# A sample's best eight found once for both halves, four gathers for eight, and the experts' first product two groups ahead

## The chip, the cores and the metric

The kernel runs on one core of a Trainium2 chip. The metric is the device time in microseconds (us) of one execution. Where the traces speak of engines, PE is TensorE (PEld its weight loads), DVE VectorE, ACT ScalarE, POOL GpSimd, and SP the engine whose queue issues most DMAs. All arithmetic is float32.

## What is computed

The input is x of 4 samples, 128 channels, 64 x 64 pixels (4096 tokens of 128 features a sample). Layer 0 normalises, makes three 1x1 convolutions and one attention over the 4096 pixels. Layer 1 first adds an attention that is a running softmax over the tokens, and then a feed-forward with 64 experts, each of which chooses its own tokens. This last part is what the change is about:

```python
logits = einsum('bsd,ed->bse', x, gate_w) + gate_b
probs = softmax(logits, axis=1)                      # over the 4096 tokens
vals, idx = top_k(probs.transpose(0, 2, 1), 8)       # each expert takes 8 tokens
gathered = take x at idx                             # (sample, 8, expert, 128)
pooled = einsum('bked,bke->bed', gathered, topv)
h = gelu([pooled, 1] @ weight1[e])                   # 128 -> 512
out = [h, 1] @ weight2[e]                            # 512 -> 128
outputs.at[idx].add(out * topv)                      # back to the chosen tokens
```

x is here the normalised token stream, and the result is added to the stream. The two weight matrices of an expert are 256 KB each, 32 MB for all 64.

## The kernel before

**Stages.** Layer 0 (its lines lie beyond L1730) fills the first 1530 us or so. Then `loop` goes over 32 blocks of 512 tokens (8 a sample) and does the running attention of one block per turn; in each turn slots named 1, 2, "D", 3, 4, "T" and "G" are places where other work is inserted. `make_plan` (from L2034) writes down by hand what goes where: the second normalisation of a finished block (`gate_norm`), its transposition (`gate_turn`), its logits (`gate_logits`), and the choice of a sample's tokens once its eight blocks are through. After the loop follow `last_choice` (for the last sample, whose last block is only just ready), `experts` (16 groups of 4 experts), and `stores`. TensorE, DVE, ACT and POOL execute in the order in which the program is written; SP executes its DMAs in the order written too, and each waits there until its target may be overwritten and until the eighth DMA before it has landed.

**A sample's choice.** The logits of a sample lie as 128 partitions x 2048: partition h x 64 + e holds expert e over one half h of the tokens. `gate_logits` (L1285 to L1293) takes the best eight of each block with the MAX8 instruction. `merge_half` (L1308) takes the best eight of those, per partition. `merge_halves` gives each partition the other half's eight: one matmul with a permutation, `swap`, exchanges the partition halves (f_pw, L1314); MAX8 over the sixteen gives the eighth best of the whole sample, the threshold, and the greatest (f_neg, L1320). `candidate_rows` searches the partition's own eight in its 2048 logits (L1326) and turns their places into row numbers of the sample's table in DRAM (L1328). `gathers` fetches them: one indirect DMA on POOL's queue for each k of 0 to 7, one row per partition (L1334). All of a half's eight are fetched, though some of them don't belong to the sample's best eight; `weigh_candidates` (L1374) gives those the weight zero. `spread_candidates` (L1382) lays the weights out as eight 128 x 64 matrices, and `pool` multiplies the eight gathered tiles with them on TensorE, accumulating (f_pp, L1406).

**The plan around it.** For the first two samples the search and the exchange stand in one turn of the loop, and the gathers go out in it and the four turns after it, at most two in a row on POOL. For the third sample there are only three turns left: its gathers stand in seven places of turns 29 to 31, four of them back to back on POOL. For the last sample, all eight stand in the last turn's "T", ahead of the outputs of the last block (L1192) on DVE. POOL makes the weight tiles of the running attention too (L1092 to L1113), once a turn.

**`last_choice`** (from L1436) fills TensorE with transpositions of earlier blocks of the stream (`fill`, L1422), which ACT or DVE copy back (`put_back`, L1434), while it normalises the last block, makes its logits, merges its best eight with the earlier ones, and pools (L1489 to L1500). It ends with the division by the softmax's sum (L1507 to L1519), which gives `pooled`.

**`experts`** keeps 21 experts' weights in the rooms that the loop has given up. For each group of four it makes the first product (`first`, f_ph, L1628), ACT copies it (f_hr, L1632), TensorE transposes it (`turn`, L1639), DVE adds the bias, ACT applies the Gelu, and the second product follows (`second`, f_eo, L1657). `first` and `second` reload what they have read (`reload1` L1564, `reload2` L1571). `turn_back` (L1589) transposes further blocks of the stream in between. The order is first(0); then for each g: turn(g), one or two turn_backs, first(g+1), second(g).

## Time and profile before

| what | us |
|---|---|
| median of 3 runs | 2319.7 (2317.64 to 2321.2) |
| the profiled execution's own time | 2321.39 |
| its span, first to last instruction | 2319.7 |
| DVE busy | 1440.9 |
| POOL busy | 193.5 |
| DMA moved | 105.82 MB |

The profile is of one execution. Its page names the busy time of each engine, a chain of work that ended last (followed back from the last instruction to what released each step), and groups of instructions by source line. Other views of the same trace list the chain by time, the instructions by time (start, duration, engine, line, output <- inputs, and in brackets how long the engine was idle before and what ended that), and busy times by stretch. "remote" in brackets, "another core or an unknown queue" in the chain, stands for a wait whose release the profile cannot put down to an instruction or a DMA that ended then.

### The profile page before, as it was taken

How to read it: one execution, taken by the hardware profiler on the slowest of the kernel's cores; microseconds unless marked ns; L12 is line 12 of the kernel's file. 1: busy time of each engine (PE TensorE's matmuls, PEld its weight loads, DVE VectorE, ACT ScalarE, POOL GpSimd, SP SyncE). 2: the span in 40 equal slices, each digit the busy share in tenths (PEclk: the TensorE clock that was granted, in tenths of full speed). 3: DMA queues.
4: the chain of work that ended last, by engine and by line, in shares of the span. 5: the costliest groups of instructions: out<-in, count | busy, mean ns of one | idle time of the engine just before them, and what ended most of it. 6: DMA issues, size and time to landing. Idle time of an engine off the chain costs nothing.

```text
span 2319.7 us, 43135 instructions
## 1 busy us (share of the span) xinstructions
PE 2247.9 (97%) x18354; PEld 1171.3 (50%) x18354; DVE 1440.9 (62%) x2325; ACT 1085.9 (47%) x1322; POOL 193.5 (8%) x364
## 2 busy tenths in 40 slices
PE   7999999999999999999999999999999999999887
PEld 3644444444444444444444444455655655656553
DVE  7666565655665565565556656567777777874533
ACT  2343334433333443334454544445665666665641
POOL 0000000000000000000000000002212222223411
PEclk9999999999999999999999999999999999999999
DMA  2100010000010000001000000011111121124578
GB/s 70 39 12 16 9 45 8 17 8 9 13 48 9 9 17 8 9 13 39 9 5 5 8 7 5 20 44 35 47 58 49 48 63 46 52 61 130 177 250 306
DMA packets 79067, 105.82 MB, mean 46 GB/s; under 512 B 9232, under 2 KB 45072, under 8 KB 78864
## 3 DMA queue, kind: packets, MB, share of 16 engines
q1 hardware_dynamic: 77264, 99.81, 14.0%
q8 instruction: 146, 2.39, 0.4%
q0 software_dynamic: 1024, 2.10, 0.4%
q10 hardware_dynamic: 576, 1.05, 0.1%
q14 instruction: 57, 0.47, 0.1%
HBM read 79.60 MB, written 17.04 MB: 42 GB/s over the span
## 4 chain that ended last, share of the span: by engine, by line
PE 88%; DVE 4%; ACT 3%; DMA 3%; issue 1%; another core or an unknown queue 1%; SPq 0%; POOL 0%; ACTq 0%; DVEq 0%; POOLq 0%
PE av L1901 37%; PE sc L1876 19%; PE f_pv L1128 9%; PE f_pk L973 8%; PE f_pt L1151 3%; PE f_po L1174 2%; PE pd L1927 1%; PE pa L1849 1%; PE pe L1823 1%; PE f_po L1186 1%; ACT f_e1a L980 1%; PE f_pl L1285 1%; DMA x<-in_x_dram 1%; PE otr L1939 1%
## 5 line engine op out<-in xcount | busy, mean ns | idle before, releaser
L1901 PE MATMUL av<-pr,am 64*128 64x512 f32 x4096 | 979.0, 592 | 1.7 <-ACT pr L1881 1.7
L1881 ACT ACTIVATE pr<-sc 128x1024 f32<-128x1024 f32 x512 | 524.2, 1024 | 783.4 <-PE sc L1876 773.5
L1888 DVE TENSOR_TENSOR acc<-acc,pr 128x1024 f32<-128x1024 f32 x480 | 586.8, 1222 | 486.7 <-ACT pr L1881 482.5
L1901 PEld LDWEIGHTS av<-pr,am 64*128 64x128 f32 x4096 | 402.6, 187 | 472.0 <-issue 458.4
L1876 PE MATMUL sc<-e,e 64*128 64x512 f32 x2048 | 536.6, 593 | 3.9 <-DMA e<-side 3.9
L1876 PEld LDWEIGHTS sc<-e,e 64*128 64x128 f32 x2048 | 202.4, 188 | 236.2 <-issue 230.3
L1128 PE MATMUL f_pv<-f_held,f_ama 128*32 128x256 f32 x4096 | 238.1, 381 | 7.0 <-ACT f_e1a L980 4.6
L973 PE MATMUL f_pk<-f_held,f_ama 128*128 128x512 f32 x512 | 234.9, 603 | 0.0
L1133 ACT ACTIVATE f_amb<-f_pv 128x1024 f32<-128x1024 f32 x128 | 130.8, 1024 | 126.3 <-PE f_pv L1128 124.2
L981 DVE TENSOR_TENSOR f_e1a<-f_e1a,f_held 128x1024 f32<-128x1024 f32 x128 | 157.0, 1228 | 48.1 <-ACT f_e1a L980 47.8
L980 ACT ACTIVATE f_e1a<-f_pk 128x1024 f32<-128x1024 f32 x128 | 130.0, 1025 | 119.3 <-PE f_pk L973 54.6
L1128 PEld LDWEIGHTS f_pv<-f_held,f_ama 128*32 128x32 f32 x4096 | 129.7, 110 | 101.4 <-issue 11.9
L982 DVE TENSOR_REDUCE f_e1a<-f_e1a 128x8 f32<-128x1024 f32 x128 | 155.3, 1218 | 3.5
L973 PEld LDWEIGHTS f_pk<-f_held,f_ama 128*128 128x128 f32 x512 | 92.5, 190 | 108.6 <-issue 101.0
L1092 POOL COPY f_held<-f_e1a 32x32 f32<-32x32 f32 x128 | 30.9, 242 | 898.2 <-DVE f_e1a L1074 560.7
L918 POOL MEMSET f_held<- 128x1024 f32 x1 | 1.0, 957 | 1037.2 <-DVE xn L1814 1037.2
L1151 PE MATMUL f_pt<-f_amb,f_held 128*32 128x128 f32 x1920 | 83.7, 278 | 0.6 <-ACT f_amb L1133 0.6
L1151 PEld LDWEIGHTS f_pt<-f_amb,f_held 128*32 128x32 f32 x1920 | 60.4, 110 | 10.3 <-issue 5.2
L1192 DVE TENSOR_TENSOR t<-t,f_po 128x512 f32<-128x512 f32 (+1 forms) x33 | 22.1, 671 | 64.2 <-PE f_po L1186 55.5
L956 ACT ACTIVATE f_xl<-t,ln_nb,ln_rs 128x128 f32<-128x128 f32 x128 | 52.8, 491 | 0.8 <-PE pa L1849 0.8
L1266 ACT ACTIVATE f_x<-t,f_gnb,f_grs 128x128 f32<-128x128 f32 x126 | 51.3, 483 | 0.4 <-DVE f_gnb L1247 0.4
L1885 DVE COPY acc<-pr 128x1024 f32<-128x1024 f32 x32 | 22.2, 694 | 39.3 <-ACT pr L1881 39.3
(275 smaller groups left out, 1789.6 us busy)
## 6 DMA issues: line engine op xcount, KB each, us to landing
f_e2a<-f_rd SPq DMA_DIRECT2D x128, 128.0 KB
xr<-in_xtok_dram SPq DMA_DIRECT2D x32, 256.0 KB
f_table<-f_x SPq DMA_DIRECT2D x62, 128.0 KB
out_dram<-t SPq DMA_DIRECT2D x14, 512.0 KB
x<-in_x_dram SPq DMA_DIRECT2D x12, 512.0 KB
e<-e SPq DMA_DIRECT2D x32, 128.0 KB
f_ama<-f_rd SPq DMA_DIRECT2D x16, 256.0 KB
f_e1b<-f_rd SPq DMA_DIRECT2D x16, 256.0 KB
```

The costliest lines, as they stand in the source:

```text
L956: nc.scalar.activation(xl[:, c, :], t[:, b * NCH + i, :], AF.Identity, bias=ln_nb[:, b, i : i + 1], scale=ln_rs[:, b, i : i + 1],)
L973: nc.tensor.matmul(pk[:, i, :], xt_at(n)[:, bass.ts(c, P)], env.wks[:, bass.ts(i, BLK)], start=True, stop=True,)
L980: nc.scalar.activation(flat, pk.rearrange("p i x -> p (i x)"), AF.Silu)
L981: nc.vector.tensor_mul(ks, ks, env.qb)
L982: nc.vector.tensor_reduce(s[:, (n % GB) * CPB + c, :], ks, AX.X, ALU.add)
L1128: nc.tensor.matmul(pv[a * CH : (a + 1) * CH, i, :], xt_at(m)[:, bass.ts(c * NA + i, CH)], env.wvs[:, bass.ts(a, HH * C)], start=True, stop ...
L1133: nc.scalar.activation(env.amb[:, bass.ts(c, HD)], pv.rearrange("p i x -> p (i x)"), AF.Silu)
L1151: nc.tensor.matmul(env.pt[i * CH : (i + 1) * CH, :], lhs, rhs, start=i not in env.begun, stop=False, skip_group_check=True,)
L1876: nc.tensor.matmul(sc[:, u, :], e2[halves[u], p, :], e1[halves[u], cols], start=True, stop=True,)
L1881: nc.scalar.activation(pr, sc, AF.Exp)
L1888: nc.vector.tensor_add(acc, acc, pr)
L1901: nc.tensor.matmul(av, am[h, j, :], pr[h, u, :], start=(j == 0), stop=(j == NCH - 1))
```

## The change

**The choice.** The row numbers are now searched before the exchange. The exchange carries values and row numbers of both halves: four matmuls with halves of the identity (`both_halves`) put both halves' sixteen values and sixteen row numbers on each partition. There MAX8 and its index search find the sample's best eight and their places among the sixteen, so both partitions of an expert know all eight; the lower partition takes the first four, the upper the last four. The row numbers of these four are picked out by comparing the places with the constants 0 to 15 (`spare(3, 48, 16)`, filled once by POOL with sixteen memsets) and summing the matches. So each partition gathers four rows, and `spread_candidates` and `pool` handle four tiles.

**The plan.** For the first three samples the search takes the slot before, and the exchange the slot after, compared with the order of the two before. The gathers of samples 0 and 1 are one a turn; sample 2's stand in four places. In `last_choice` put_back(8) and put_back(5) go from DVE to ACT, and the matmul of the softmax's sum (f_pq) is issued after the first half of the last pooling matmuls.

**The experts.** first(0) and first(1) come ahead of the loop over groups, and first(g+2) takes the place of first(g+1). f_hr, of which there was one, has two places by turns.

```diff
         def merge_half(b, count):
             st = sel[b]
-            st["both"] = both = small_tile(b, "both", 24, bufs=1)
+            st["both"] = both = small_tile(b, "both", 16, bufs=1)
             nc.vector.max(out=both[:, 0:8], in_=st["cand"][:, : count * 8])
+        def both_halves(tile_, what):
+            pw = sm(what, 2, tile_.shape[1])
+            for h in range(2):
+                for to in range(2):
+                    nc.tensor.matmul(
+                        pw[to * E : (to + 1) * E, h], ident[:, h * E : (h + 1) * E], tile_,
+                        start=True, stop=True,
+                    )
+            return pw
+        def candidate_rows(b, count):
+            st = sel[b]
+            both = st["both"]
+            ci = small_tile(b, "ci", 8, dtype=U32, bufs=1)
+            nc.vector.max_index(out=ci, in_max=both[:, 0:8], in_values=flat_lg(b, 0, count))
+            nc.vector.tensor_scalar(
+                out=both[:, 8:16], in0=ci, scalar1=env.base[:, b : b + 1], scalar2=None,
+                op0=ALU.add,
+            )
         def merge_halves(b):
             st = sel[b]
-            both = st["both"]
-            pw = sm(f"f_pw_{b}", 8)
-            nc.tensor.matmul(pw, env.swap, both[:, 0:8], start=True, stop=True)
-            nc.vector.tensor_copy(both[:, 8:16], pw)
-            st["top"] = top = small_tile(b, "top", 8)
-            nc.vector.max(out=top, in_=both[:, 0:16])
-            nc.vector.tensor_copy(both[:, 16:17], top[:, 7:8])
+            pw = both_halves(st["both"], f"f_pw_{b}").rearrange("p s (v k) -> p v s k", v=2)
+            found = spare(3, 0, 32).rearrange("p (v s k) -> p v s k", v=2, s=2)
+            nc.vector.tensor_copy(found, pw)
+            first8 = spare(3, 32, 16).rearrange("p (v k) -> p v k", v=2)
+            st["top"] = top = first8[:, 0]
+            vals, rows16 = spare(3, 0, 16), spare(3, 16, 16)
+            nc.vector.max(out=top, in_=vals)
             st["neg"] = neg = small_tile(b, "neg", 1)
             nc.vector.tensor_scalar_mul(neg, top[:, 0:1], -1.0)
+            pos = small_tile(b, "ci", 8, dtype=U32, bufs=1)
+            nc.vector.max_index(out=pos, in_max=top, in_values=vals)
+            nc.vector.tensor_copy(first8[:, 1], pos)
+            st["own"] = own = small_tile(b, "own", 2, 4, bufs=1)
+            for h in range(2):
+                half = slice(h * E, (h + 1) * E)
+                nc.vector.tensor_copy(own[half], first8[half, :, 4 * h : 4 * h + 4])
+            st["src"] = src = small_tile(b, "src", 5, bufs=1)
+            nc.vector.tensor_copy(src[:, 0:4], own[:, 0])
+            nc.vector.tensor_copy(src[:, 4:5], top[:, 7:8])
+            hit = spare(2, 0, 64).rearrange("p (k j) -> p k j", k=4)
+            nc.vector.tensor_tensor(
+                hit, own[:, 1].unsqueeze(2).to_broadcast([P, 4, 16]),
+                spare(3, 48, 16).unsqueeze(1).to_broadcast([P, 4, 16]), ALU.is_equal,
+            )
+            nc.vector.tensor_tensor(
+                hit, hit, rows16.unsqueeze(1).to_broadcast([P, 4, 16]), ALU.mult,
+            )
+            rowf = small_tile(b, "rowf", 4, bufs=1)
+            nc.vector.tensor_reduce(rowf, hit, AX.X, ALU.add)
+            st["at"] = at = small_tile(b, "at", 4, dtype=I32, bufs=1)
+            nc.vector.tensor_copy(at, rowf)
...
-            for k in range(8):
-                nc.tensor.matmul(pp, g_at(k), dd[:, k, :], start=(k == 0), stop=(k == 7))
+            for k in range(4):
+                nc.tensor.matmul(pp, g_at(k), dd[:, k, :], start=(k == 0), stop=(k == 3))
...
-            pw = sm("f_pw1", 8)
-            nc.tensor.matmul(pw, env.swap, late, start=True, stop=True)
+            pw = both_halves(late, "f_pw1")
...
+            put_back(8, act, 2)
+            put_back(5, act)
+            dd = spread_candidates(weigh_candidates(b))
...
-            put_back(8, dve, 2)
...
-            for kk in range(4, 8):
-                nc.tensor.matmul(pp, g_at(kk), dd[:, kk, :], start=False, stop=False)
...
-            put_back(5, dve)
-            pq = ps.tile([P, BLK], F32, tag="t", name="f_pq3")
-            nc.tensor.matmul(pq[:, 0:1], env.pair, sums[:, 0:1], start=True, stop=True)
+                if h == 0:
+                    pq = ps.tile([P, BLK], F32, tag="x", name="f_pq3")
+                    nc.tensor.matmul(pq[:, 0:1], env.pair, sums[:, 0:1], start=True, stop=True)
...
             first(0)
+            first(1)
...
-                if g + 1 < EG:
-                    first(g + 1)
+                if g + 2 < EG:
+                    first(g + 2)
...
-                at(i, 2, merge_halves, b)
-                at(i, 3, candidate_rows, b, NBLK)
+                at(i, 2, candidate_rows, b, NBLK)
+                at(i, 3, merge_halves, b)
...
-                for k in range(8):
-                    at(i + (k + 1) // 2, 3 if k % 2 else "G", gathers, b, k, k + 1)
+                for k in range(4):
+                    at(i + k, "G", gathers, b, k, k + 1)
...
-            at(NB - 3, 1, merge_halves, last)
-            at(NB - 3, 2, candidate_rows, last, NBLK)
-            slots = [(NB - 3, 3), (NB - 3, 4), (NB - 3, "G"), (NB - 2, 1), (NB - 2, 3),
-                     (NB - 2, 4), (NB - 2, "G"), (NB - 1, 1)]
+            at(NB - 3, 1, candidate_rows, last, NBLK)
+            at(NB - 3, 2, merge_halves, last)
+            slots = [(NB - 3, 4), (NB - 2, 1), (NB - 2, 4), (NB - 1, 1)]
...
-            at(NB - 1, "T", gathers, B - 1, 0, 8)
+            at(NB - 1, "T", gathers, B - 1, 0, 4)
```

## The prediction, made before the changed kernel was run

> **What bounds the kernel now.** I read the page's busy shares first, then the chain of work that ended last by stretches, then the timeline of the stretch that looked odd, then windows over the experts' stage.

> ```profile
> PE 2247.9 (97%) x18354; PEld 1171.3 (50%) x18354; DVE 1440.9 (62%) x2325; ACT 1085.9 (47%) x1322; POOL 193.5 (8%) x364
> ...
> PE 88%; DVE 4%; ACT 3%; DMA 3%; issue 1%; another core or an unknown queue 1%; SPq 0%; POOL 0%; ACTq 0%; DVEq 0%; POOLq 0%
> ```

> TensorE bounds all but the end; nothing of the change lies before 1830 us, so the averages say little. The chain in the stretch the change touches:

> ```profile
> 2004.45 1.93 PE f_pp L1406 x16
> ...
> 2135.30 2.59 PE f_pp L1406 x16
> ...
> 2169.23 0.81 issue
> 2170.03 0.61 PE f_pv L1128 x2
> 2170.81 1.19 issue
> ...
> 2190.97 15.68 another core or an unknown queue
> 2206.67 1.02 ACT t L1434
> ```

> The pooling matmuls (f_pp) are on the chain, so halving them counts. The big piece is 15.68 us in which the chain waits for something the profile cannot name. The timeline there:

> ```profile
> 2195.05 0.94 POOL L1334 DMA_INDIRECT f_e1b<-f_table,f_at  x1 [12.28 <-DVE f_neg L1320]
> ...
> 2203.73 0.75 DVE L1192 TENSOR_TENSOR t<-t,f_po 128x256 f32<-128x256 f32 x2 [8.69 <-remote]
> 2203.80 0.95 POOL L1334 DMA_INDIRECT f_e1b<-f_table,f_at  x1 [0.30 <-remote]
> ...
> 2206.67 1.01 ACT L1434 COPY t<-f_etb 128x1024 f32<-128x1024 f32 x1 [15.71 <-remote]
> ```

> DVE's L1192 waits only for the matmuls L1186, which end at 2196.05; ACT's L1434 only for the first eight transposes L1422, over by about 2197.5. Both start 7 to 9 us late, and the eight gathers of the last sample (2195.05 to 2204.75, one each 1.25 us) fill exactly that time. The same shows smaller at 2163.68 to 2169.25: four gathers, and DVE idles 2.84 us for f_pl, TensorE 0.81 us. Over the whole span "remote" ends a wait five times, all in these two stretches: none beside the earlier pairs of gathers (1853 to 2098), none in the saturated DMA after 2234. So while a train of gathers queues behind weight loads, TensorE's completions seem to reach the others late.

> ```profile
> 2195.00:2206.00 11.00, 5.11 (x64) 3.64 (x54) 2.17 (x11) 0.00 (x0) 8.57 (x10) 0.79 0.86 314
> 2222.00:2234.00 12.00, 11.61 (x158) 8.42 (x159) 5.32 (x8) 7.29 (x14) 2.65 (x14) 0.86 0.76 247
> 2234.00:2250.00 16.00, 14.55 (x220) 9.50 (x223) 3.31 (x17) 6.65 (x15) 0.76 (x5) 1.00 1.05 390
> 2250.00:2258.00 8.00, 7.75 (x114) 4.97 (x106) 1.87 (x7) 3.22 (x7) 0.30 (x2) 1.00 1.03 354
> 2258.00:2285.00 27.00, 22.86 (x244) 11.82 (x246) 1.12 (x5) 6.58 (x15) 0.76 (x5) 1.00 1.04 383
> ```

> The last two columns are DMA share and GB/s. The experts' stage is a weight stream: full from 2234 on, but only 247 GB/s in its first 12 us, because a slot is reloaded only after its matmul has read it.

> **The change, part by part.** The profiled execution took 2321.39 us, its span 2319.7, with 1.7 around it; the median of the three runs is also 2319.7, 1.7 below the profiled time. I work out a difference and take it from the median.

> Pooling, eight matmuls to four. Samples 0, 1, 2 show groups of 16 passes at 1.93, 2.59 and 2.00 us, all on the path (for sample 2, f_pooled waits 1.63 us for them and starts the last sample's search). Half: 0.97 + 1.30 + 1.00 = **-3.2**. The last sample's second half (L1496, 1.00 us) ends at 2217.57, beside the copy f_e2b that ends at 2217.54, so it is costed at nothing here.

> Exchange of the halves, one f_pw matmul to four. The row is 0.32 us for two passes (1836.96); now eight passes with half the columns. No row has this shape: the 32 passes of f_etr take 0.48 us (0.015 each), f_pp's take 0.12. Eight cost 0.12 to 0.96, so -0.2 to +0.64 a time. f_pl, which also has 64 columns but streams 256, takes 0.145, and 16 must stream faster, so I take 0.065, +0.2 a time for three samples and +0.3 in the last choice, where DVE's L1462 waits for it: **+0.9** (-0.8 to +2.6).

> DVE's list: thirteen small instructions where four were, and the index search moved ahead of the exchange, past L981 and L982. The four took 2194.42 to 2195.04, a pitch of 0.2 us, so thirteen take 2.5, and 1.8 is new. In sample 0 the chain from 1847.14 to 1855.5 runs through ACT; DVE idles 0.58 before L981 and 1.85 at 1853.65, and ACT uses L1040's result at 1851.48, 2.5 us after it is made. That covers both; samples 1 and 2 look alike (2024 to 2032; 2153 to 2155, where DVE idles 2.3). Cost 0, up to +0.5 each if a cover is short. The spreads shrink by 0.3 us each, hidden too.

> Sample 2's gathers, now at most two in a row instead of four. The stall of 0.81 + 1.19 us around 2169 to 2172 should mostly go; I take **-1.3** (0 to -2.0), since ACT's table load would start at 2169.4 rather than 2170.71, and everything after hangs on it. Late next is then f_pv itself.

> The last sample's choice. New: TensorE's f_pw waits for the row numbers, which end at 2194.31; it stood at 2193.34. Behind it queue the products and outputs, which need 2.7 us from there (2193.34 to 2196.05), so they end at 2197.2, and ACT's first eight transposes at 2198.6. DVE's thirteen run 2194.9 to 2197.4, L1192 follows unheld. The gathers start 0.7 later, as they did after the row numbers (2194.31 to 2195.05), so at 2198.1, and the fourth ends at 2198.1 + 3 x 1.25 + 0.95 = 2202.8. ACT's copy was let go 1.9 us after the last gather: 2204.7 instead of 2206.67, -1.9. If nothing is held it starts at 2198.7, -8.0. If the hold is as long as before from its first gather (11.6 us), 2209.7, +3.1. I take **-3.0**: near the first, as the row is nearest, a little below because DVE's part is out before the gathers begin.

> [...] A rule that speaks against the change: a gather took 3.08 us at 2178.44 instead of 0.95, beside a DVE instruction of 2.32 us. [...]

> The handover. put_back(8) and put_back(5) leave DVE (1.22 and 0.68 us) for ACT, which is free from 2218.54 to 2221.76 and needs 1.6. Then f_e2b's copy starts at 2216.95, not 2217.13 (-0.2), and f_pq after the first half of L1500 (1.10 us): -0.5. **-0.7** (0 to -1.0), until put_back(8), which frees the buffer of f_ph, is late: it ends near 2219.6, f_ph starts near 2219.9.

> Experts' first product two groups ahead. first(1) runs while ACT copies f_hr, so eight reloads of 256 KB stand in SP's queue from 2221.6 to 2225.4 instead of four, and the next eight follow before those have flowed (2 MB at 385 GB/s is 5.4 us; a group takes TensorE 3.4). The stream then runs full from its start: 12 us x (385 - 247) / 385 = **-4.3**. With 350 GB/s at first it is -3.3; if the dip at 2250 closes too, -5.0. Every load is still read in the order in which it is issued, so the end of the stage moves with the stream.

> Sum: -3.2 + 0.9 - 1.3 - 3.0 - 0.7 - 4.3 = -11.6, so 2319.7 - 11.6 = **2308.1 us**.

> **The rivals.**
> *The hold goes altogether.* For it: pairs of gathers in the quiet stretch hold nothing. Against: weights still load at 314 GB/s then. Last choice -8.0 instead of -3.0: 2303.1.
> *The hold belongs to the weight loads, not to the number of gathers.* For it: it ends as the DMA falls quiet after 2205. Then the last choice is +3.1 and sample 2 gains nothing: 2308.1 + 6.1 + 1.3 = 2315.5.
> *The stream starts no earlier*, because first(2), behind two turn-backs, is again late, or the first reloads wait in SP's queue: without the 4.3, 2312.4.
> *Slower: TensorE stands behind the index search.* f_pw used to need a maximum only; now it needs the 2.3 us search, in TensorE's order ahead of everything. For it: DVE is 62% busy. Against: the row numbers should be there 1 to 2 us before f_pw in samples 0 to 2. Each further us of lateness costs up to 1 us in four samples; it beats the gains only from about 4 us each (4 x 4 = 16 against 11.6 + 4.6).

> **How the numbers follow.** 4.6 us (0.2%) is about what a measurement of this kernel tells from no change. Forecast 0.53; hold gone 0.17; hold unshortened 0.13; stream no earlier 0.10; slower 0.05; 0.02 for what I do not see. Forecast, hold gone and stream are faster by over 4.6 (below 2315.1), with a third of the unshortened hold: 0.84. Same takes the rest of that and the unforeseen, 0.11; slower 0.05. The forecast's own ends, from the bounds above, are about 2303 and 2315; down to the hold gone with some gain more, up to the hold unshortened: 2301 to 2316.

> **What would show it.** Right: f_pp in groups of 8; ACT's first L1434 copy less than 10 us after the table load before it and no "remote" of 8 us on DVE; 385 GB/s in the first 12 us of the stage; the last weight some 10 us earlier. Wrong: f_pw idle for DVE's row numbers in samples 0 to 2; ACT's copy still waiting 15 us; the first 12 us at 250 GB/s; L1040 arriving after ACT's table load.

## The result: no difference that can be measured

The changed kernel took 2320.8 us (median of 12 runs, 2318.0 to 2326.4), the kernel before, beside it, 2320.3 us (12 runs). The ratio is 1.0005, with a 95% interval of 0.9995 to 1.0015. The forecast was 2308.1 us, its range 2301 to 2316; the result lies above it. The profiled execution has a span of 2322.0 us, 2.3 longer than the one of before.

The profile page of the changed kernel, its busy times and the shares of the chain by engine:

```profile
PE 2247.8 (97%) x18352; PEld 1168.5 (50%) x18352; DVE 1444.6 (62%) x2361; ACT 1086.4 (47%) x1324; POOL 175.9 (8%) x364
...
PE 86%; DVE 6%; ACT 3%; DMA 3%; issue 1%; SPq 0%; POOL 0%; another core or an unknown queue 0%; ACTq 0%; DVEq 0%; POOLq 0%
```

Two things moved: the unknown wait is gone from the chain (1% before, 0% now), and DVE has 6% of it instead of 4%. So something was won where it was looked for, and something was lost to DVE. The place of the loss is found by taking the same TensorE instructions (f_pk L973, f_po L1186) in both traces and writing down where their distance jumps. The second column of measurements is explained with the experiments: there both kernels ran on another chip.

| stretch | predicted, us | first chip | another chip |
|---|---|---|---|
| exchange of sample 0 | +0.2 | +5.6 | +5.7 |
| pooling of sample 0 | -1.0 | -1.4 | -1.4 |
| exchange of sample 1 | +0.2 | +7.1 | +5.7 |
| on to sample 1's pooling | -1.3 | -3.5 | -4.6 |
| exchange of sample 2 | +0.2 | +3.7 | +4.5 |
| sample 2's gathers and pooling | -2.3 | -1.6 | -0.7 |
| last choice, from the last L1186 to the first f_ph | -3.4 | -6.7 | -0.6 |
| experts, from the first f_ph to the first f_sct | -4.3 | +0.2 | -1.4 |
| stores | 0 | 0 | +0.3 |
| sum | -11.7 | +3.4 | +7.4 |

(The traces also differ by 1.1 us at the start of sample 0's choice, before anything of the change, the changed kernel being earlier; the spans differ by the sum less that. The predicted column is rounded row by row; the prediction's own sum is -11.6. The row of sample 2's gathers and pooling contains 1.0 us by which f_pw of the last sample waits for its row numbers, L1320 at 2202.10, which the prediction had put into the last choice.) Three exchanges that were to cost 0.6 us cost 16.4. The timeline of the changed kernel at samples 0 and 2:

```profile
1838.29 2.27 DVE L1330 FIND_INDEX8 f_ci<-f_both,f_lg 128x8 uint32<-128x2048 f32 x1
...
1840.60 0.23 DVE L1331 TENSOR_SCALAR f_both<-f_ci,f_base 128x8 f32<-128x8 uint32 x1
...
1841.77 0.65 PE L1291 MATMUL f_pl<-f_e1b,f_gws 128*64 128x256 f32 x4
...
1845.51 0.47 DVE L1295 TENSOR_SCALAR f_lg<-f_pl,f_gbs 128x256 f32<-128x256 f32 x1
...
1846.04 0.62 PE L1320 MATMUL f_pw<-f_both,ident 128*64 128x16 f32 x8 [3.62 <-DVE f_lg L1295]
...
1846.59 5.00 PE L1128 MATMUL f_pv<-f_held,f_ama 128*32 128x256 f32 x64
...
2156.68 0.23 DVE L1331 TENSOR_SCALAR f_both<-f_ci,f_base 128x8 f32<-128x8 uint32 x1
...
2156.97 0.62 PE L1320 MATMUL f_pw<-f_both,ident 128*64 128x16 f32 x8 [2.56 <-DVE f_both L1331]
...
2157.51 3.12 PE L1128 MATMUL f_pv<-f_held,f_ama 128*32 128x256 f32 x32
```

In sample 0 the row numbers (L1331) are ready at 1840.83, before TensorE gets to f_pw. Still f_pw waits 3.62 us, and what ends the wait is L1295, the instruction with which DVE reads f_pl. f_pl and f_pw both ask the pool for the tag `sm`, and that tag has one buffer: f_pw may not be written until DVE has read f_pl, and DVE has the search and four passes of L981 and L982 (4.9 us) ahead of that. Sample 1 shows the same 3.62 us at 2027.36. In sample 2 it is the search itself: DVE's 2.3 us L1399 stands ahead of it, and f_pw waits 2.56 us for L1331.

The wait is not all. f_pv behind it took 5.00 us for 64 passes, where the profile of before has 3.66:

```profile
1843.41 3.66 PE L1128 MATMUL f_pv<-f_held,f_ama 128*32 128x256 f32 x64
```

Windows of the changed kernel around the three waits (length; then busy us of TensorE and its weight loads, DVE, ACT, POOL; the granted clock, the DMA share and GB/s):

```profile
1842.60:1845.90 3.30, 0.00 (x0) 0.00 (x0) 3.27 (x4) 0.00 (x0) 0.00 (x0) 1.00 0.39 117
1845.90:1849.30 3.40, 3.26 (x36) 1.85 (x40) 2.67 (x16) 0.00 (x0) 0.00 (x0) 0.51 0.02 5
2026.90:2033.70 6.80, 6.34 (x64) 3.28 (x68) 2.99 (x17) 1.02 (x1) 0.00 (x0) 0.50 0.01 2
2153.20:2156.60 3.40, 1.20 (x16) 0.55 (x8) 3.40 (x3) 1.54 (x3) 0.00 (x0) 0.99 0.00 0
2156.60:2160.00 3.40, 3.04 (x32) 1.70 (x36) 3.14 (x15) 0.00 (x0) 0.00 (x0) 0.50 0.15 40
```

The clock also explains the row "on to sample 1's pooling", where the changed kernel wins 2 to 3 us more than pooling should give. The kernel before ran the end of sample 1's pooling (from 2135.30) and what follows at half clock, behind a wait for a DMA; the changed kernel, in the same place, did not. First a window of before, then one of the changed kernel:

```profile
2136.50:2139.90 3.40, 3.40 (x48) 3.13 (x50) 0.36 (x2) 2.29 (x6) 0.00 (x0) 0.50 0.75 185
...
2144.80:2148.20 3.40, 3.40 (x105) 3.33 (x108) 0.73 (x4) 3.40 (x9) 0.51 (x3) 1.00 0.67 160
```

In a later run of the same code (the changed kernel with the experts one group ahead, below) the clock fell in that place too, from 2145.28, and there the row is the predicted -1.3.

In the last choice the timeline shows what was won:

```profile
2204.91 0.74 DVE L1192 TENSOR_TENSOR t<-t,f_po 128x256 f32<-128x256 f32 x2
...
2205.74 0.94 POOL L1372 DMA_INDIRECT f_e1b<-f_table,f_at  x1 [15.60 <-DVE t L1192]
...
2205.89 1.01 ACT L1472 COPY t<-f_etb 128x1024 f32<-128x1024 f32 x1 [6.30 <-PE f_etb L1460]
...
2211.49 0.69 DVE L1285 COPY f_e1b<-f_gtr 128x512 f32<-128x512 f32 x1 [2.85 <-remote]
```

DVE's L1192 is not held, nor is ACT's copy; both slip through before the train of gathers is under way (the first gather starts at 2205.74, the copy 0.15 us later). A hold of "remote" of 2.85 us comes later, at f_gtr's copy, and ends 1.0 us after the last gather.

### The profile page after: what moved, and what is told of

It reads as the page before. It is cut to its first block, busy times and chain, and to the rows that moved or that the text cites. A ratio compares the mean times of both kernels' runs of the same rounds, so it can differ in the third digit from the quotient of the medians.

```text
span 2322.0 us, 43150 instructions
## 1 busy us (share of the span) xinstructions
PE 2247.8 (97%) x18352; PEld 1168.5 (50%) x18352; DVE 1444.6 (62%) x2361; ACT 1086.4 (47%) x1324; POOL 175.9 (8%) x364
## 3 DMA queue, kind: packets, MB, share of 16 engines
q0 software_dynamic: 512, 1.05, 0.2%
q10 hardware_dynamic: 576, 1.05, 0.1%
## 4 chain that ended last, share of the span: by engine, by line
PE 86%; DVE 6%; ACT 3%; DMA 3%; issue 1%; SPq 0%; POOL 0%; another core or an unknown queue 0%; ACTq 0%; DVEq 0%; POOLq 0%
PE av L1939 36%; PE sc L1914 18%; PE f_pv L1128 9%; PE f_pk L973 8%; PE f_pt L1151 3%; PE f_po L1174 2%; PE pd L1965 1%; DMA x<-in_x_dram 1%; ACT f_e1a L980 1%; PE pa L1887 1%; PE pe L1861 1%; PE f_po L1186 1%; DVE f_e1a L981 1%; DVE f_e1a L982 1%; PE f_pl L1291 1%
## 5 line engine op out<-in xcount | busy, mean ns | idle before, releaser
L1128 PE MATMUL f_pv<-f_held,f_ama 128*32 128x256 f32 x4096 | 242.7, 387 | 5.5 <-ACT f_e1a L980 4.5
L973 PE MATMUL f_pk<-f_held,f_ama 128*128 128x512 f32 x512 | 234.9, 603 | 0.0
L981 DVE TENSOR_TENSOR f_e1a<-f_e1a,f_held 128x1024 f32<-128x1024 f32 x128 | 157.5, 1231 | 46.6 <-ACT f_e1a L980 46.2
L1128 PEld LDWEIGHTS f_pv<-f_held,f_ama 128*32 128x32 f32 x4096 | 131.3, 111 | 102.2 <-issue 15.1
L982 DVE TENSOR_REDUCE f_e1a<-f_e1a 128x8 f32<-128x1024 f32 x128 | 155.3, 1218 | 3.5
L973 PEld LDWEIGHTS f_pk<-f_held,f_ama 128*128 128x128 f32 x512 | 92.5, 190 | 109.1 <-issue 101.4
L1192 DVE TENSOR_TENSOR t<-t,f_po 128x512 f32<-128x512 f32 (+1 forms) x33 | 22.1, 671 | 55.6 <-PE f_po L1186 55.6
```

Source lines behind the costliest of these rows:

```text
L973: nc.tensor.matmul(pk[:, i, :], xt_at(n)[:, bass.ts(c, P)], env.wks[:, bass.ts(i, BLK)], start=True, stop=True,)
L981: nc.vector.tensor_mul(ks, ks, env.qb)
L982: nc.vector.tensor_reduce(s[:, (n % GB) * CPB + c, :], ks, AX.X, ALU.add)
L1128: nc.tensor.matmul(pv[a * CH : (a + 1) * CH, i, :], xt_at(m)[:, bass.ts(c * NA + i, CH)], env.wvs[:, bass.ts(a, HH * C)], start=True, stop ...
```

## Experiments: the waits of TensorE

**Another buffer for f_pw.** The only edit to the changed kernel:

```diff
-        def both_halves(tile_, what):
-            pw = sm(what, 2, tile_.shape[1])
+        def both_halves(tile_, what, other=False):
+            w = tile_.shape[1]
+            if other:
+                pw = ps.tile([P, BLK], F32, tag="x", name=what)[:, : 2 * w]
+                pw = pw.rearrange("p (s v) -> p s v", s=2)
+            else:
+                pw = sm(what, 2, w)
...
-            pw = both_halves(st["both"], f"f_pw_{b}").rearrange("p s (v k) -> p v s k", v=2)
+            pw = both_halves(st["both"], f"f_pw_{b}", b < 2).rearrange("p s (v k) -> p v s k", v=2)
```

> The changed kernel, but f_pw of samples 0 and 1 goes into the PSUM buffer x instead of sm. Theory (one buffer): f_pw waits 3.62 us because sm still holds f_pl, which DVE empties only behind four passes of L981 and L982 and the 2.3 us search; the idle TensorE then loses its clock for one to two periods of 3.41 us. Then the waits and the half clock after 1845 and 2026 go, and the time falls by 5 to 6.5 us a sample, 10 to 13 together: about 2309. Rival (the search): f_pw waits for the row numbers; they end at 1840.83 and TensorE gets there near 1842.4, but if DVE's lateness is what counts the next wait on DVE takes the place of this one: 2318 to 2321.

Measured: 2311.6 us, 0.9955 of the kernel before (0.9942 to 0.9969). Its timeline at sample 0:

```profile
1841.72 0.65 PE L1291 MATMUL f_pl<-f_e1b,f_gws 128*64 128x256 f32 x4
...
1842.20 0.36 PE L1325 MATMUL f_pw<-f_both,ident 128*64 128x16 f32 x8
...
1842.50 3.66 PE L1128 MATMUL f_pv<-f_held,f_ama 128*32 128x256 f32 x64
...
1845.46 0.47 DVE L1295 TENSOR_SCALAR f_lg<-f_pl,f_gbs 128x256 f32<-128x256 f32 x1
...
1846.54 0.66 PE L965 MATMUL f_ltr<-ident,f_xl 128*128 128x128 f32 x4 [0.38 <-DVE f_e1b L1345]
```

f_pw runs at once, 3 us before DVE reads f_pl, and f_pv takes 3.66 us again. The jump of the distance is now +0.7 us in either sample, instead of +5.6 and +7.1; 0.38 of it is the next user of the buffer `x`, f_ltr, waiting for DVE to read f_pw. So what held f_pw in samples 0 and 1 was the buffer, and not DVE's added work as such.

**Sample 2's exchange one slot later**, and in `x` too:

```diff
-            pw = both_halves(st["both"], f"f_pw_{b}", b < 2).rearrange("p s (v k) -> p v s k", v=2)
+            pw = both_halves(st["both"], f"f_pw_{b}", b < 3).rearrange("p s (v k) -> p v s k", v=2)
...
-            at(NB - 3, 2, merge_halves, last)
+            at(NB - 3, 3, merge_halves, last)
```

> The same for all of samples 0 to 2, and sample 2's exchange one slot later (slot 3 for slot 2), behind f_pl. Theory (TensorE stands behind the search in sample 2, 2.56 us, and behind that one period of half clock, f_pv 3.12 for 1.93 us): a further 3 to 4 us, about 2305.5. Rival: the gathers of sample 2 then start later and its pooling waits for them, or DVE's exchange pushes L1122 and the logits back, so that the gain is eaten: as the kernel with the other buffer, 2309.

Measured: 2304.6 us, 0.9937 (0.9924 to 0.9950) of the kernel before. At sample 2:

```profile
2137.57 2.32 DVE L1404 SCALAR_TENSOR_TENSOR f_lg<-f_lg,f_ce 128x2048 f32<-128x2048 f32 x1
...
2139.87 2.29 DVE L1335 FIND_INDEX8 f_ci<-f_both,f_lg 128x8 uint32<-128x2048 f32 x1
...
2142.20 0.23 DVE L1336 TENSOR_SCALAR f_both<-f_ci,f_base 128x8 f32<-128x8 uint32 x1
...
2143.29 0.36 PE L1325 MATMUL f_pw<-f_both,ident 128*64 128x16 f32 x8
...
2143.58 1.93 PE L1128 MATMUL f_pv<-f_held,f_ama 128*32 128x256 f32 x32
```

The row numbers are ready 0.9 us before f_pw, and in this trace no window of half clock is left before the last choice. Here the search is covered, as the prediction had assumed, and the time is 3.5 us below the forecast. But that the two come so close is luck. Its trace is 16.8 us shorter than that of before, and 5.1 of them lie ahead of sample 0, where nothing was changed: the clock was halved there three times for 3.41 us in the trace of before, and never in this one. From sample 0 on the difference is 11.7 us, made of other parts than the forecast's: samples 0 to 2 -4.3 (predicted -4.0), the last choice -7.1 (predicted -3.4), the experts -0.5 (predicted -4.3).

**How much of the loss is the clock.** Unneeded matmuls ahead of f_pw keep TensorE busy without shortening its wait:

```diff
         def merge_halves(b):
             st = sel[b]
+            if b < 2:
+                warm = ps.tile([P, BLK], F32, tag="x", name=f"f_warm_{b}")
+                for _ in range(6):
+                    nc.tensor.matmul(warm, ident, t[:, 0:4, :].rearrange("p i x -> p (i x)"),
+                                     start=True, stop=True)
```

> The changed kernel with six unneeded 128x512 matmuls ahead of f_pw of samples 0 and 1, inside the time that TensorE waits anyway (six take about 2.8 of the 3.6 us). Theory (half of the loss is the wait, a third the clock that TensorE loses by idling): f_pw starts as before, but the clock stays at 1.00 and f_pv behind it takes 3.66 us instead of 5.00 and 6.47, so 1.3 and 2.8 us go: about 2317. Rival (the clock falls for another reason, such as time or power): 2321, the dips at 1845 and 2026 still there.

The size was wrong: each of these matmuls is two passes, and the twelve took 5.42 us, so f_pw came 1.7 us after DVE had read f_pl. Yet f_pv took 3.66 us and no half clock was left at either sample, so that the jumps stayed at +5.7 us each. The ratio was 1.0041 (1.0027 to 1.0055), the same that the changed kernel has on another chip where the kernel before takes as long (below). With `range(3)`:

> The changed kernel with three unneeded 128x512 matmuls (six passes of 0.45 us, 2.7 us) ahead of f_pw of samples 0 and 1. With six the clock held at 1.00, but their twelve passes (5.42 us) outlasted the wait, so f_pw came 1.7 us late and nothing was won in sample 0. Theory: three end inside the wait, f_pw starts with DVE's L1295 as in the changed kernel, f_pv behind it takes 3.66 us, and samples 0 and 1 cost 4.2 us each where they cost 5.6 and 7.1: 2 to 4 us below the changed kernel. Rival: 2.7 us of work in a window are too few, the clock falls all the same: the same time as the changed kernel.

```profile
1842.18 0.65 PE L1291 MATMUL f_pl<-f_e1b,f_gws 128*64 128x256 f32 x4
...
1842.76 2.84 PE L1341 MATMUL f_warm<-t,ident 128*128 128x512 f32 x6
...
1845.92 0.47 DVE L1295 TENSOR_SCALAR f_lg<-f_pl,f_gbs 128x256 f32<-128x256 f32 x1
...
1846.45 0.41 PE L1320 MATMUL f_pw<-f_both,ident 128*64 128x16 f32 x8 [0.85 <-DVE f_lg L1295]
...
1846.79 3.66 PE L1128 MATMUL f_pv<-f_held,f_ama 128*32 128x256 f32 x64
```

The end of the wait is still L1295, but the clock holds, and a sample costs 4.0 us instead of 5.6 and 7.1 (5.7 in both samples on another chip). So in the trace useless work made this stretch faster. In the kernel's time it is not clear of noise: 1.0028 (1.0018 to 1.0037) of the kernel before, beside 1.0041 (1.0024 to 1.0057) for the changed kernel on another chip of the same speed, and the intervals overlap. The size fits the clock in every trace that has this wait of 3.62 us: 4.0 us where no half clock follows (here), 5.6 to 5.7 where it follows for 3.41 us (four samples of three traces), 7.0 and 7.1 where it follows for 6.83 us (two samples of two traces). So of a sample's loss about 3.4 us are the wait, 1.5 to 3.0 the clock, and 0.7 what the other buffer also left.

## Experiments: the hold in the last choice

The prediction rested on a hold that the gathers, or the weight loads beside them, put on whoever waits for TensorE. Two kernels were to tell these apart, both from the kernel before:

```diff
-            at(NB - 1, "T", gathers, B - 1, 0, 8)
+            at(NB - 1, "T", gathers, B - 1, 0, 4)
```

> The kernel before with four of the last sample's eight gathers left out (the other four tiles keep the rows of sample 2, so the pooled values of the last sample are not the reference's). Only the stretch from 2190 to 2215 is looked at. Theory (the train of gathers holds back what waits for TensorE): with four, DVE's L1192 and ACT's first L1434 copy start when the shorter train is over, about 4 x 1.25 = 5 us earlier, L1192 near 2199 and L1434 near 2201.7 instead of 2203.73 and 2206.67. Rival (the weight loads hold it): both as before, within 1 us.

and, in the other, every `load_into` of `load_rooms` without its DMA (each call there gets `skip=True`):

```diff
-        def load_into(slot):
+        def load_into(slot, skip=False):
...
-            nc.sync.dma_start(out=slot, in_=fw[e])
+            if not skip:
+                nc.sync.dma_start(out=slot, in_=fw[e])
```

> The kernel before with the loads of load_rooms left out (14 experts compute with what lies in their rooms, so the output is not the reference's), all eight gathers kept: no weights move beside them. Only the stretch up to 2215 is looked at. Theory (gathers alone): L1192 still starts 7 to 9 us late. Rival (weight loads, or gathers queued behind them): L1192 starts within 1 us of the end of L1186, near 2196.5, and the first L1434 copy near 2198.

In both (2312.9 and 2314.7 us, one run each), L1192 began 1.12 us after the start of L1186, unheld. That looked like a decision for the weight loads, but for one thing: the kernel before took 2309.0 us beside these runs, not 2320.4. So it was run for its own trace, with the changed kernel and the same two again.

> The kernel before itself, for its trace on the chip of these runs: on one chip it took 2320.4 us, on another 2309.0, and there two kernels with its last choice showed no hold (DVE's L1192 1.1 us after the end of f_gtr's work, not 8.7). If the hold is there, about 2320 and L1192 7 to 9 us late; if it is not, about 2309 and L1192 within 1.5 us of L1186.

> The changed kernel beside the kernel before on this chip. Theory (the change loses 12 to 16 us to TensorE's waits in samples 0 to 2 on any chip, and gains 7 in the last choice only where the hold is): where the kernel before shows the hold, the same time as before; where it does not, slower by 0.3 to 0.5%. Rival (the hold has nothing to do with it): the same ratio, 1.0005, in both.

> The kernel before with four of the last sample's eight gathers left out, again (its pooled values of the last sample are not the reference's). Where the kernel before shows the hold here: L1192 about 5 us earlier than there if the train of gathers holds it, the same if the weight loads do. Where there is no hold: nothing to tell.

> The kernel before with the loads of load_rooms left out, again (14 experts compute with what lies in their rooms). Where the kernel before shows the hold here: L1192 still 7 to 9 us late if the gathers alone hold it, within 1.5 us of L1186 if it takes weight loads beside them. Where there is no hold: nothing to tell.

The timeline of the kernel before, unchanged, on this chip:

```profile
2193.03 1.06 PE L1186 MATMUL f_po<-f_e1b 128*32 128x128 f32 x32
2193.09 0.94 POOL L1334 DMA_INDIRECT f_e1b<-f_table,f_at  x1 [12.28 <-DVE f_neg L1320]
...
2194.16 0.75 DVE L1192 TENSOR_TENSOR t<-t,f_po 128x256 f32<-128x256 f32 x2 [1.07 <-PE f_po L1186]
2194.34 0.95 POOL L1334 DMA_INDIRECT f_e1b<-f_table,f_at  x1 [0.30 <-PE f_po L1186]
...
2195.15 1.02 ACT L1434 COPY t<-f_etb 128x1024 f32<-128x1024 f32 x1 [6.14 <-PE f_etb L1422]
```

All eight gathers and all weight loads are there, at the same pace (each gather 1.25 us after the one before; 351 GB/s from 2193 to 2203, where the first chip moved 334 from 2195 to 2205), and nothing is held: L1192 starts with the end of L1186, the first copy 2.1 us after L1186 began (11.7 on the first chip). The last choice takes 15.75 us there, 25.56 on the first chip. The four-gathers and no-loads kernels (2311.7 and 2308.2 us, one run each) have L1192 unheld too and tell nothing more. On this chip the changed kernel was slower: 2317.7 us against 2309.5, a ratio of 1.0041 (1.0024 to 1.0057).

So the hold was seen on one chip only. The kernels ran on four: on one the kernel before takes 2320.4 us (2320.3 in the first result, so I count that to it), on the other three 2309.0, 2309.5 and 2309.4. On the first, both traces with the eight-gather train show the hold (that of before, and that of two groups ahead alone: L1192 8.7 and 7.2 us after L1186's start); on two of the others, three traces with that train show none (the kernel before itself on one, the kernel without loads on both). With four gathers the sign is f_gtr's copy: in the four traces of the first chip it starts 1.3 to 2.1 us after the end of its matmuls and never before the last gather is over; in all twelve traces of the other three chips it starts 0.04 us after them, in ten of these with the last gather still to end. With the clock behind it, which differs too, the hold is worth 9.8 us to the kernel before and 3.8 to the changed one (18.91 against 15.11). That the two kernels came out equal on the first chip is thus chance: the sum of a loss of about 7 to 8 us, which the other chip shows whole, and a gain of 6 that only the first gives. What the delay is made of stays open, as neither of the two kernels fell on that chip. But weight loads are not needed for the smaller hold, of which the prediction told, at sample 2's four gathers in the trace of before:

```profile
2168.30 0.95 POOL L1334 DMA_INDIRECT f_e1b<-f_table,f_at  x1 [0.30 <-issue]
...
2170.05 0.48 DVE L1289 TENSOR_SCALAR f_lg<-f_pl,f_gbs 128x256 f32<-128x256 f32 x1 [2.84 <-remote]
```

SP issued no weight load between 2154.75 and 2177.30. The 0.70 MB that moved from 2163.5 to 2169.3 are about what these gathers (64 KB each) and the four f_e2a loads issued beside them (128 KB each) come to.

## Experiments: the experts' two groups ahead

Taken back from the changed kernel, and put alone into the kernel before (there with the two places for f_hr):

```diff
             first(0)
-            first(1)
...
-                if g + 2 < EG:
-                    first(g + 2)
+                if g + 1 < EG:
+                    first(g + 1)
```

> The changed kernel, but the experts' first product one group ahead as before. If two groups ahead is worth the 4.3 us of the prediction and something else ate it: 2325. If the weight stream ends no earlier for it (its first reload at 2224.61 and its last landing at 2289.9 are 65.3 us apart, against 65.7 before): 2320 to 2322.

> The kernel before, with the experts' first product two groups ahead and nothing else of the change. By the prediction's step 2316.0; if the stage's length is the stream's 43 pairs of loads at its full rate plus a start that two groups ahead only shifts, 2319 to 2321.

Measured, on the first chip: without it 2325.1 us, 1.0013 (1.0003 to 1.0023) of before, where the changed kernel has 1.0005; alone 2319.7 us, 0.9995 (0.9986 to 1.0004). The same taken from the kernel with the later exchange, beside that kernel:

> The kernel with the later exchange, but the experts' first product one group ahead as before. Prediction's step: 4.3 us more than with two ahead. What the two traces of before and of two ahead alone showed (1014 against 821 KB per us-third in the first 12 us, 1.5 us of a full stream): 1.3 to 1.9 us more.

(The figures in that text are sums of GB/s over four 3 us slices.) Measured: 0.9995 (0.9985 to 1.0005) against 0.9977 (0.9967 to 0.9987), medians 2306.7 and 2303.4. So it gains 1.2, 1.9 and 4.2 us by the ratios, with intervals about as wide as the differences; in the traces the stage shortens by 1.3 (70.09 to 68.78), 0.2 and 2.7 us. All point the same way; the prediction's 4.3 is their upper end. The other traces of this case narrow it: the stage takes 70.1 to 72.7 us, 71.3 in the mean, in the six traces with one group ahead and all loads, and 68.3 to 70.9, 69.4 in the mean, in the ten with two. That is 1.9 us. Why it is less is in the windows of the stage's first 12 us, 3 us each. With two groups ahead alone:

```profile
2220.14:2223.14 3.00, 3.00 (x26) 1.56 (x27) 0.39 (x2) 1.50 (x3) 0.00 (x0) 1.00 0.25 74
2223.14:2226.14 3.00, 3.00 (x51) 1.83 (x50) 1.02 (x2) 2.66 (x5) 0.35 (x3) 1.00 0.89 255
2226.14:2229.14 3.00, 3.00 (x52) 2.04 (x50) 1.42 (x3) 1.80 (x4) 2.22 (x12) 1.00 0.91 297
2229.14:2232.14 3.00, 3.00 (x52) 2.04 (x50) 2.48 (x2) 1.84 (x4) 0.07 (x1) 1.00 1.05 392
```

The same four slices in the kernel before:

```profile
2220.55:2223.55 3.00, 2.22 (x14) 1.31 (x15) 0.00 (x0) 1.78 (x2) 0.00 (x0) 0.72 0.29 88
2223.55:2226.55 3.00, 3.00 (x36) 2.05 (x38) 1.42 (x3) 1.62 (x5) 0.00 (x0) 0.71 0.78 262
2226.55:2229.55 3.00, 3.00 (x50) 1.99 (x42) 1.42 (x3) 1.71 (x4) 2.00 (x11) 1.00 0.71 232
2229.55:2232.55 3.00, 3.00 (x56) 2.25 (x50) 1.40 (x2) 1.73 (x4) 0.65 (x4) 1.00 0.82 240
```

The first two, the start of the stream, are no better with more reloads waiting (88 and 262 GB/s without, 74 and 255 with them); only the last two are. By these rows it is (254.5 - 205.5) x 12 / 385 = 1.5 us, not 4.3. (The clock differs in the first two, 0.72 against 1.00, so not all of the stage's 1.3 us need be the order's doing.) In the changed kernel the first slice has 13 GB/s, because the first product runs at a granted clock of 0.50 and frees its first weights 1.9 us after it begins, instead of 1.1.

## The version that beats both

The kernel with the later exchange was run again away from the first chip, and with sixteen repeated transposes in the last choice, meant to keep the clock up there:

```diff
             fill(8, "kv")
+            again(8)
+            again(8)
...
             fill(11, "kv", 1)
+            again(10)
+            again(11)
```

> The kernel with the later exchange, and in the last choice sixteen transposes repeated (four twice behind fill(8), eight once behind fill(11)) where TensorE waits for DVE. Theory (the 13.65 us of half clock from 2193.59 come from idling at 2191 to 2193 and cost 3 to 4 us: f_pp 1.94 for 1.0, f_pc 0.64 for 0.39, the last f_pp 2.2 for 1.1, f_ph's first reload 0.8): about 2301. Rival (the clock falls anyway, or repeats of 128x128 transposes do not count): the repeats stand on the path with up to 1.9 us, 2305 to 2307.

> The kernel with f_pw in x and sample 2's exchange one slot later, on the chip of these runs. On the chip with the hold it was 0.9937 of the kernel before. Theory: 6.7 us of that are the last choice that the hold no longer stretches; on a chip without the hold 0.996 to 0.9985 (4 to 9 us: pooling 3, sample 2's gathers 2, experts 1.3). Rival (all of it is independent of the hold): 0.9937 there too.

> The same with the sixteen repeated transposes in the last choice. Theory (they keep the clock up in the last choice and for the first product): 1 to 3 us below the kernel without them on the same chip. Rival (without the hold TensorE idles less and keeps its clock anyway, so the repeats only cost): the same or up to 2 us above.

With the repeats: 0.9971 (0.9960 to 0.9983) in the first of these runs; beside the kernel without them, 0.9981 (0.9971 to 0.9990) against 0.9977 (0.9967 to 0.9987). They win nothing: the last choice takes 15.99 us with them and 16.05 without, and the clock still falls at 2204.5, just ahead of f_ph. The later exchange beats the kernel before on either kind of chip, 0.9937 with the hold and 0.9977 without, where the changed kernel has 1.0005 and 1.0041. By these ratios more than half of its 0.6% on the first chip is the hold.

## Why the prediction was wrong, step by step

- **The step that failed** is "the index search moved ahead of the exchange ... Cost 0, up to +0.5 each if a cover is short", with "one f_pw matmul to four". I asked whether DVE's and ACT's own waits would cover 1.8 us of new DVE work. I did not ask what f_pw waits for in its new slot: the single `sm` buffer that f_pl takes just ahead of it. Cost: 12.7 us in samples 0 and 1, 1.4 with another buffer.
- **The rival that came true in part** was given 0.05, "TensorE stands behind the index search". Its counter-argument, that the row numbers would be there 1 to 2 us before f_pw, held for samples 0 and 1, where it did not matter, and failed for sample 2. Its price, at most 1 us for each us of lateness, left out the clock: 2.56 us late cost 3.7, 3.62 late cost 5.6 and 7.1. Its threshold of 4 us in each of four samples was thus too high: 9.8 us of waits in three samples cost 16.4.
- **Pooling** (-3.2) was right: groups of 8 passes at 1.10 us where 16 took 1.93 to 2.59. But the 2.59 was no row to halve: its passes ran in part at half clock, and what the changed kernel wins there beyond pooling is the clock. **The passes of f_pw** (+0.2 each) are at most 0.7 with the buffer's own wait. **Sample 2's gathers** (-1.3) measured -1.7.
- **DVE's pitch**: I took 0.2 us an instruction from the rows, 2.5 us for thirteen. In the last choice they took from 2202.56 to 2205.00, 2.44 us: the rows were right.
- **The gathers beside L1192**: whether they would be slow there, as the gather of 3.08 us beside a DVE instruction of 2.32 us was, was not put to the test: the first gather started at 2205.74, 0.09 us after L1192 had ended, and the four took 0.94 to 0.96 us each.
- **The last choice** (-3.4 with f_pw and the handover) measured -6.7 on the chip of the profile. The order was foreseen, gathers after the outputs, but not its effect: I let ACT's copy wait for the last gather, and it slipped through before the train. On a chip without the hold the term is -0.6, so the gain is luck of the chip; that the hold could go with one chip was in none of the cases.
- **The experts** (-4.3) were mis-sized: the shortfall of the first 12 us was taken as the order's doing, and more than half of it is the start of the stream. The pairs of traces show 0.2 to 2.7, all of them together 1.9.

## What to carry to other kernels

When a producer is moved on an in-order engine, list for its new place not only its inputs but its output buffer: who filled that buffer last, which engine empties it, and what stands in that engine's queue. A stall of TensorE of some 3 us cost one and a half to two times its length here, as the clock was halved behind it; whether for 3.41 or 6.83 us changed from run to run. And a wait that the profile cannot name should be looked for on a second chip before a gain is built on it.

## What the runs showed of the hardware that was not expected

- Three unneeded matmuls (2.84 us) inside a wait took a sample's loss from 5.6 to 7.1 us down to 4.0, because the granted clock stayed at 1.00. Stretches of 3.41 us in which TensorE was busy for less than half lost the clock 30 times of 30, one of them with 1.20 us busy of 3.40.
- On one chip of four, what waited for TensorE started 7 to 9 us late beside a train of eight indirect gathers and 1.3 to 2.7 us late beside one of four; on the other three no trace shows a delay in these places. The same program, with the same gathers each 1.25 us apart, was traced on one of these: its last choice is 9.8 us shorter there, which is most of the 11 us (2309 against 2320) by which the kernel before is faster.
